# A graph layer's weight stage: seven combined block products replaced by four plain projections

## The chip, the core and the metric

The kernel runs on one core of a Trainium2 chip. The metric is the time of one execution on the device in microseconds (us); the times shown are medians over runs. The engines are named as the profile names them: PE is TensorE (matmuls), PEld its weight loads, DVE is VectorE, ACT is ScalarE, POOL is GpSimd, and SP is the engine that issues the DMA transfers. "L279" is line 279 of the kernel before.

## The reference

The input is 64 graphs of 256 nodes with 768 features, and for each a 256 x 256 matrix of 0 and 1. Each graph goes through a layer norm with a ReLU and then through one graph layer, whose result is added to the input:

```python
h = jnp.maximum(_layernorm(x, axis=-1), 0.0)
adj = heads.astype(hs.dtype)
radj = jnp.swapaxes(adj, 1, 2)
deg, rdeg = adj.sum(-1), radj.sum(-1)          # deg_c, rdeg_c: at least 1
ctx = jnp.matmul(adj, hs @ Wadj.T + badj) / deg_c[..., None]
ctx = ctx + jnp.matmul(radj, hs @ Wrev.T + brev) / rdeg_c[..., None]
ctx = ctx + hs @ Wself.T + bself
agg = jnp.einsum('bij,bijr->bir', adj, E[rels])
rel = agg @ Wr.T + br * deg[..., None]
...
return ctx + rel                                # x + this
```

With entries of 0 and 1 the relation terms come down to rows that depend on the degrees alone, so they become one small extra matmul. What is left is, for each graph, three 256 x 768 matrices (forward neighbour means, reverse neighbour means, and h itself), each times a 768 x 768 weight matrix, summed. This last part is called the weight stage below.

## The kernel before

The kernel works through the 64 graphs (`B`) in a software pipeline. `step(t)` works on three graphs at once: graph M = t is in the weight stage, A = t + 1 in the neighbour sums, and N = t + 2 is loaded and normalised. Each engine carries out its instructions in the order in which `step` writes them; the scheduler does not move them. A graph's 256 nodes are C = 2 blocks of 128 partitions, its 768 features are F = 6 blocks of 128, and FH = 3, HO = 384 are the halves.

For graph N, `load` (L159 to L163) fetches `x`, `adj` (both directions) and `xT`, an x that comes already transposed from the host. `degrees` (L171, ACT) casts adj to `a` and sums its rows; `statistics` (L181 to L194, DVE, with one small power on POOL, L184) makes mean, reciprocal deviation and degrees in `cols`. `spread` (L201) transposes `cols` on PE, copies it twice on ACT (`tokT`, `line`), and sends four rows through DRAM (`d<-line`, L208) and back to all partitions (`row<-d`, L210). `normalise` (L223 to L227) writes h as a pair of float32r tiles, `hi` and its remainder `lo`, with DVE and ACT taking turns.

For graph A, `aggregate(A, f)` makes one of six neighbour sums: four float32r matmuls of 512 columns (L248) into one of the two banks of `pa`, and a DVE multiply by the reciprocal degrees (L253) that reads the bank and writes two thirds of X's block f. `self_features` (L239 on POOL, L240 on ACT) normalises `xT` with `row` and writes the last third of X. X has two buffers, `pa` has two banks, `row`, `xT`, `adj`, `hi` and `lo` have one buffer each.

For graph M the weight stage treats X (2 x 2 blocks) times W (2 x 2 blocks) with seven block products in place of eight. `combine_weights` (L107 to L110, DVE, once) forms sums of weight blocks, `combine_left` (L270 to L273, POOL, every step) forms sums of blocks of X in place. Each `product` is 9 float32 matmuls of 384 columns (L279), in the trace two records each; four of the seven carry one more float32r matmul with `rows` and `tokT` (L285). Three products accumulate further onto a bank that another has already filled. `add_out` (L294) adds a bank to x, the last add (L351) takes one bank twice. Between the products `step` places the neighbour sums of A in three pairs. `prepare_rows` (once) builds `rows` out of biases and relation weights.

A flag counts entries of adj other than 0 and 1; a general path, not taken here, would then run after the main one.

Of the kernel before, what the change touches and what calls it, by code (L numbers as in the profile page):

```python
# [9 lines left out]
F32 = mybir.dt.float32  # L10
F32R = mybir.dt.float32r
# [3 lines left out]
ALU = mybir.AluOpType  # L15
AX = mybir.AxisListType

P = 128
# [5 lines left out]
def kernel(  # L24
# [24 lines left out]

    nc = tc.nc
    B, L, H = x.shape
    NREL = e_t.shape[1]
# [2 lines left out]
    F = H // P  # L59
    FH = F // 2  # L60
    HO = H // 2
# [17 lines left out]
    def main_path(main: ExitStack):  # L79
        pool1 = main.enter_context(tc.tile_pool(name="pool1", bufs=1))  # L80
# [3 lines left out]
        ps2 = main.enter_context(tc.tile_pool(name="ps2", bufs=2, space=bass.MemoryType.PSUM))  # L84
        ps1 = main.enter_context(tc.tile_pool(name="ps1", bufs=1, space=bass.MemoryType.PSUM))

        w11, w21, w22, t1, t2, t3, t4 = (
            pool1.tile([P, FH, 3, HO], F32, name=n) for n in ("w11", "w21", "w22", "t1", "t2", "t3", "t4")
        )
        rows = pool1.tile([P, 4, HO], F32R, name="rows")  # L90
        tok = [pool1.tile([P, C, NROW], F32, name=f"tok{i}") for i in range(2)]
        cols = [pool1.tile([P, C, 64], F32, name=f"cols{i}") for i in range(2)]

        def load_weights():
            def block(t, k, n):
                for s, w in enumerate((wadj_t, wrev_t, wself_t)):
                    v = w.rearrange("(f p) o -> p f o", p=P)
                    nc.sync.dma_start(t[:, :, s, :], v[:, k * FH : (k + 1) * FH, ts(n, HO)])

            block(w11, 0, 0)  # L100
            block(w21, 1, 0)
            block(t3, 0, 1)
            block(w22, 1, 1)

        def combine_weights():

            nc.vector.tensor_sub(t1, t3, w11)  # L107
            nc.vector.tensor_sub(t2, w22, t1)
            nc.vector.tensor_sub(t4, w21, t2)
            nc.vector.tensor_sub(t3, w22, t3)  # L110

        def prepare_rows():


            eT = pool1.tile([P, NREL], F32, name="eT")
            nc.sync.dma_start(eT, e_t)
            wr = [pool1.tile([P, H], F32, tag=f"hl{k}", name=f"wr{k}") for k in range(2)]
            nc.sync.dma_start(wr[0], wr_t)
            nc.sync.dma_start(wr[1], wrr_t)
            brow = pool3.tile([P, H], F32, tag="x", name="brow")  # L120
            nc.vector.memset(brow, 0.0)
            pick = pool1.tile([P, 2, P], F32, tag="s1", name="pick")
            nc.vector.memset(pick, 0.0)
            for q in range(4):
                nc.sync.dma_start(brow[q * 32 : q * 32 + NROW, :], bias)
                nc.vector.tensor_copy(pick[:, 0, q * 32 + 3 : q * 32 + 4], eT[:, 1:2])
                nc.vector.tensor_copy(pick[:, 1, q * 32 + 4 : q * 32 + 5], eT[:, NBASE + 1 : NBASE + 2])
            hi = pool1.tile([P, H], F32R, tag="hx", name="rows_hi")
            for n in range(2):
                pr = ps2.tile([P, 512], F32, tag="pa", name=f"pr{n}")  # L130
                for k in range(2):
                    nc.tensor.matmul(pr[:, :HO], pick[:, k, :], wr[k][:, ts(n, HO)], start=(k == 0), stop=(k == 1))
                nc.vector.tensor_add(brow[:, ts(n, HO)], brow[:, ts(n, HO)], pr[:, :HO])
            nc.vector.tensor_copy(hi, brow)
            hi = hi.bitcast(F32)
            nc.vector.tensor_sub(brow, brow, hi)
            nc.vector.tensor_copy(rows, brow[:, :1].unsqueeze(2).to_broadcast([P, 4, HO]))
            for q in range(4):
                at = slice(q * 32, (q + 1) * 32)
                src = (hi if q % 2 == 0 else brow)[at, :]  # L140
                zero = pick[at, 0, 16:17].to_broadcast([32, HO])
                c = q // 2

                for k, part in enumerate(((0, 0, 1), (1, 0, 1), (1, 1, 1), None)):
                    if part is None:
                        nc.vector.tensor_scalar(
                            rows[at, k, :], src[:, ts(1, HO)], 1.0 if c == 0 else -1.0, None, op0=ALU.mult
                        )
                    elif part[0] == c:
                        nc.vector.tensor_copy(rows[at, k, :], src[:, ts(part[1], HO)])  # L150
                    else:
                        nc.vector.tensor_copy(rows[at, k, :], zero)

        S = [{} for _ in range(B)]

# [98 lines left out]
                s["X"][:, f, 0:2, :].rearrange("p s i -> p (s i)"), pa, s["row"][:, 2:4, :].rearrange("p s i -> p (s i)")  # L254
            )

        def left(b):
            X = S[b]["X"]

            def block(c, k):  # L260
                return X[:, k * FH : (k + 1) * FH, :, ts(c, P)]

            return block(0, 0), block(0, 1), block(1, 0), block(1, 1)

        def combine_left(b):

            s = S[b]
            a11, a12, a21, a22 = left(b)
            s["s1"] = pool1.tile([P, FH, 3, P], F32, tag="s1", name=f"s1_{b}")
            nc.gpsimd.tensor_tensor(s["s1"], a21, a22, op=ALU.add)  # L270
            nc.gpsimd.tensor_tensor(a21, a11, a21, op=ALU.subtract)  # L271
            nc.gpsimd.tensor_tensor(a11, s["s1"], a11, op=ALU.subtract)  # L272
            nc.gpsimd.tensor_tensor(a12, a12, a11, op=ALU.subtract)  # L273

        def product(b, ps, l, w, start, stop=True, row=None):
            n = 0
            for f in range(FH):
                for k in range(3):
                    nc.tensor.matmul(  # L279
                        ps, l[:, f, k, :], w[:, f, k, :], start=(start and n == 0),  # L280
                        stop=(stop and row is None and n == 3 * FH - 1), skip_group_check=not start,
                    )
                    n += 1
            if row is not None:
                nc.tensor.matmul(  # L285
                    ps, S[b]["tokT"], rows[:, row, :], start=False, stop=stop, skip_group_check=not start
                )

        def bank(b, name, pool=None):
            return (pool or ps1).tile([P, 512], F32, tag=name, name=f"{name}_{b}")[:, :HO]  # L290

        def add_out(b, c, n, ps):
            o = S[b]["x"][:, c, ts(n, HO)]
            nc.vector.tensor_add(o, ps, o)  # L294

        def step(t):

            M, A, N = t, t + 1, t + 2
            has_m, has_a, has_n = 0 <= M < B, 0 <= A < B, 0 <= N < B
            if has_n:  # L300
                load(N)
            if t == -2:
                load_weights()
                prepare_rows()
                combine_weights()
            if has_a:
                new_left(A)
            if has_m:
                a11, a12, a21, a22 = left(M)
                p1 = bank(M, "p1", ps2)  # L310
                product(M, p1, a11, w11, True)
            if has_a:
                aggregate(A, 0)
                aggregate(A, 1)
            if has_m:
                add_out(M, 0, 0, p1)
                p2 = bank(M, "p2")
                product(M, p2, a12, w21, True, row=0)
                combine_left(M)
            if has_a:  # L320
                aggregate(A, 2)
                aggregate(A, 3)
                self_features(A)
            if has_n:
                degrees(N)
                statistics(N)
            if has_m:
                add_out(M, 0, 0, p2)
                p4 = bank(M, "p4")
                product(M, p4, a22, t4, True, row=1)  # L330
            if has_a:
                aggregate(A, 4)
                aggregate(A, 5)
            if has_m:
                add_out(M, 1, 0, p4)
                p5 = bank(M, "p5")
                product(M, p5, S[M]["s1"], t1, True, row=2)
            if has_n:
                spread(N)
            if has_m:  # L340
                add_out(M, 1, 1, p5)
                product(M, p1, a11, t2, False)
                add_out(M, 0, 1, p1)
            if has_n:
                normalise(N)
            if has_m:
                product(M, p5, a12, w22, False, row=3)
                add_out(M, 0, 1, p5)
                product(M, p1, a21, t3, False)
                o = S[M]["x"][:, 1, :].rearrange("p (n o) -> p n o", n=2)  # L350
                nc.vector.tensor_add(o, p1.unsqueeze(1).to_broadcast([P, 2, HO]), o)  # L351
                nc.sync.dma_start(out_v[M], S[M]["x"])

        for i in range(2):
# [171 lines left out]
```

## Time and profile before

| | |
|---|---|
| median of 3 runs | 3097.47 us |
| all runs | 3095.09 to 3099.42 us |
| the profiled execution's own time | 3099.42 us |
| its span, first to last instruction | 3097.4 us |
| mean granted clock of PE | 0.992 |
| float32 product records on PE (L279) | 8064, spread over three groups, 486 to 487 ns each |
| neighbour-sum matmuls (L248) | 1536, 398 to 422 ns each |
| row matmuls (L285) | 256, 633 ns each |
| combine_left on POOL (L270 to L273) | 256, 2618 to 2664 ns each |
| self_features on POOL (L239) | 128, 3652 ns each |
| DMA, mean over the span | 74 GB/s |

The durations of PE are those of single records. Records overlap, so these durations add up to more than the time PE is busy; what a record adds to a stream is the distance from its start to the next one's, and the chain of waits shows pieces that are free of overlap. In that chain each piece begins where the engine or transfer that released it ended. The time of an execution (3099.42) is 2.0 us longer than the span of its instructions (3097.4).

### The profile page before, as it was taken

What the parts mean: (1) busy time and instruction counts of PE and PEld (TensorE: products, weight loads), DVE (VectorE), ACT (ScalarE), POOL (GpSimd) and SP (SyncE); (2) the same over time, 40 slices, a digit from 0 to 9 for tenths busy, and PEclk for the clock granted to TensorE, in tenths of its full rate; (3) what the DMA queues carried; (4) which work ended last, traced back from release to release, by engine and by line L of the source; (5) the groups of instructions that cost most, each with busy time, mean ns of one, the idle gap of its engine ahead of it and who ended that gap; (6) DMA issues with size and microseconds to landing.
All of it is one profiled execution on the core that took longest, in us unless ns stands there. A gap on an engine that the chain in (4) does not pass through costs nothing.

```text
span 3097.4 us, 24497 instructions
## 1 busy us (share of the span) xinstructions
PE 3023.2 (98%) x9930; PEld 1875.4 (61%) x9930; DVE 1015.1 (33%) x1963; ACT 339.6 (11%) x833; POOL 1185.2 (38%) x454
## 2 busy tenths in 40 slices
PE   1999999999999999999999999999999999999999
PEld 1566666666666666666666666666666666666665
DVE  4433333333233333333333332332333333333331
ACT  0111011011011011110110110110111101101100
POOL 1434334344344344343343343443443443433432
PEclk7999999999999999999999999999999999999999
DMA  4222212212212212212222122122122122222210
GB/s 154 78 72 72 78 64 80 79 61 82 79 55 80 87 55 79 79 65 79 72 72 79 62 82 79 61 83 79 55 78 89 55 79 75 68 79 72 72 62 21
DMA packets 118029, 227.96 MB, mean 74 GB/s; under 512 B 6020, under 2 KB 60292, under 8 KB 117912
## 3 DMA queue, kind: packets, MB, share of 16 engines
q1 hardware_dynamic: 117912, 226.36, 21.3%
q8 instruction: 79, 1.29, 0.2%
q14 instruction: 38, 0.31, 0.0%
HBM read 175.74 MB, written 50.59 MB: 73 GB/s over the span
## 4 chain that ended last, share of the span: by engine, by line
PE 97%; issue 2%; DVE 0%; POOL 0%; DMA 0%; ACT 0%; SPq 0%; POOLq 0%; ACTq 0%
PE p L279 84%; PE pa L248 11%; PE p L285 1%; PE pt L201 0%; POOL xT L239 0%; DVE lo L227 0%; DMA row<-d 0%; DVE hx L223 0%; ACT hi L226 0%; ACT a L171 0%; POOL cols L184 0%; ACT X L240 0%; DMA d<-line 0%; DVE X L253 0%; DVE x L351 0%
## 5 line engine op out<-in xcount | busy, mean ns | idle before, releaser
L279 PE MATMUL p<-w,X 128*128 128x384 f32 x3456 | 1148.3, 487 | 0.0
L279 PE MATMUL p<-t,X 128*128 128x384 f32 x3456 | 1145.9, 486 | 0.0
L279 PEld LDWEIGHTS p<-w,X 128*128 128x128 f32 x3456 | 657.7, 190 | 448.2 <-issue 2.4
L279 PEld LDWEIGHTS p<-t,X 128*128 128x128 f32 x3456 | 650.5, 190 | 423.9
L272 POOL TENSOR_TENSOR X<-s,X 128x1152 f32<-128x1152 f32 x64 | 170.5, 2664 | 1159.0 <-PE p L279 1159.0
L253 DVE TENSOR_TENSOR X<-pa,row 128x512 f32<-128x512 f32 x384 | 259.0, 688 | 762.3 <-PE pa L248 760.5
L239 POOL TENSOR_TENSOR xT<-xT,row 128x1536 f32<-128x1536 f32 x128 | 467.5, 3652 | 12.2 <-DMA row<-d 7.2
L279 PE MATMUL p<-t,s 128*128 128x384 f32 x1152 | 381.9, 486 | 0.0
L294 DVE TENSOR_TENSOR x<-p,x 128x384 f32<-128x384 f32 x384 | 209.3, 552 | 379.2 <-PE p L279 347.3
L248 PE MATMUL pa<-a,hi 128*128 128x512 f32 x768 | 323.9, 422 | 2.1 <-ACT hi L226 2.1
L248 PE MATMUL pa<-a,lo 128*128 128x512 f32 x768 | 305.6, 398 | 3.4 <-DVE lo L227 3.4
L279 PEld LDWEIGHTS p<-t,s 128*128 128x128 f32 x1152 | 218.7, 190 | 141.3
L273 POOL TENSOR_TENSOR X<-X 128x1152 f32<-128x1152 f32 x64 | 170.0, 2655 | 322.9 <-PE p L279 322.9
L270 POOL TENSOR_TENSOR s<-X 128x1152 f32<-128x1152 f32 x64 | 167.6, 2618 | 320.5 <-PE p L279 306.5
L227 DVE SCALAR_TENSOR_TENSOR lo<-hx,cols,hi 128x768 fp32r<-128x768 f32 x128 | 134.0, 1047 | 451.6 <-ACT hi L226 451.6
L240 ACT ACTIVATE X<-xT 128x1536 f32<-128x1536 f32 x64 | 94.9, 1484 | 1619.6 <-POOL xT L239 1619.6
L248 PEld LDWEIGHTS pa<-a,hi 128*128 128x128 f32 x768 | 145.5, 189 | 54.8 <-ACT hi L226 3.1
L271 POOL TENSOR_TENSOR X<-X 128x1152 f32<-128x1152 f32 x64 | 168.1, 2626 | 5.0
L248 PEld LDWEIGHTS pa<-a,lo 128*128 128x128 f32 x768 | 145.4, 189 | 39.6 <-DVE lo L227 4.7
L285 PE MATMUL p<-rows,tokT 128*128 128x384 f32 x256 | 162.1, 633 | 0.0
L190 DVE TENSOR_SCALAR tok<-tok 128x4 f32<-128x4 f32 x64 | 10.9, 170 | 404.0 <-ACT a L171 404.0
L226 ACT ACTIVATE hi<-hx,cols 128x768 fp32r<-128x768 f32 x128 | 119.9, 936 | 107.9 <-DVE hx L223 107.9
(52 smaller groups left out, 787.7 us busy)
## 6 DMA issues: line engine op xcount, KB each, us to landing
x<-in_x_dram SPq DMA_DIRECT2D x64, 768.0 KB
xT<-in_x_t_dram SPq DMA_DIRECT2D x64, 768.0 KB
out_dram<-x SPq DMA_DIRECT2D x64, 768.0 KB
adj<-in_adj_dram SPq DMA_DIRECT2D x64, 512.0 KB
row<-d SPq DMA_DIRECT2D x64, 512.0 KB
d<-line SPq DMA_DIRECT2D x128, 2.0 KB
w<-in_Wadj_dram SPq DMA_DIRECT2D x3, 576.0 KB
w<-in_Wrev_dram SPq DMA_DIRECT2D x3, 576.0 KB
```

The lines of the kernel that those rows point to most:

```text
L226: nc.scalar.activation(s["hi"][:, c, :], hx[:, c, :], AF.Copy, scale=rstd)
L227: nc.vector.scalar_tensor_tensor(s["lo"][:, c, :], hx[:, c, :], rstd, s["hi"][:, c, :].bitcast(F32), op0=ALU.mult, op1=ALU.subtract)
L239: nc.gpsimd.tensor_tensor(xT, xT, row[:, k : k + 1, :].to_broadcast([P, F, L]), op=op)
L248: nc.tensor.matmul(pa, s[part][:, c, ts(f, P)], s["a"][:, c, :, :].rearrange("p s i -> p (s i)"), start=(k == 0), stop=(k == 2 * C - 1),)
L253: nc.vector.tensor_mul(s["X"][:, f, 0:2, :].rearrange("p s i -> p (s i)"), pa, s["row"][:, 2:4, :].rearrange("p s i -> p (s i)"))
L270: nc.gpsimd.tensor_tensor(s["s1"], a21, a22, op=ALU.add)
L271: nc.gpsimd.tensor_tensor(a21, a11, a21, op=ALU.subtract)
L272: nc.gpsimd.tensor_tensor(a11, s["s1"], a11, op=ALU.subtract)
L273: nc.gpsimd.tensor_tensor(a12, a12, a11, op=ALU.subtract)
L279: nc.tensor.matmul(ps, l[:, f, k, :], w[:, f, k, :], start=(start and n == 0), stop=(stop and row is None and n == 3 * FH - 1), skip_group ...
L285: nc.tensor.matmul(ps, S[b]["tokT"], rows[:, row, :], start=False, stop=stop, skip_group_check=not start)
L294: nc.vector.tensor_add(o, ps, o)
```

## The change

The block scheme of seven products goes. The three weight matrices are loaded whole (`w_sb`), in three transfers and not twelve, and no sums of weight blocks or of blocks of X are formed. For each of the 2 x 2 output blocks, `project` runs one row matmul and then 18 float32 matmuls into a bank of `po` (two banks), and adds the bank to x once. `rows` becomes 2 x 768 wide, without signs and half-width pieces. In `step`, the neighbour sums stand in two groups of three, and `spread` and `normalise` follow each other behind the third projection. The short name of the change speaks of neighbour sums in two float32r passes, transposes laid out by the host and row values spread by DMA; these parts are in both kernels, word for word.

```diff
-        w11, w21, w22, t1, t2, t3, t4 = (
-            pool1.tile([P, FH, 3, HO], F32, name=n) for n in ("w11", "w21", "w22", "t1", "t2", "t3", "t4")
-        )
-        rows = pool1.tile([P, 4, HO], F32R, name="rows")
+        w_sb = [pool1.tile([P, F, H], F32, name=f"w{k}") for k in range(3)]
+        rows = pool1.tile([P, 2, H], F32R, name="rows")
...
+            for t, w in zip(w_sb, (wself_t, wadj_t, wrev_t)):
+                nc.sync.dma_start(t, w.rearrange("(f p) o -> p f o", p=P))
-        def combine_weights():
-            nc.vector.tensor_sub(t1, t3, w11)
-            nc.vector.tensor_sub(t2, w22, t1)
-            nc.vector.tensor_sub(t4, w21, t2)
-            nc.vector.tensor_sub(t3, w22, t3)
...
-            nc.vector.tensor_copy(rows, brow[:, :1].unsqueeze(2).to_broadcast([P, 4, HO]))
             for q in range(4):
                 at = slice(q * 32, (q + 1) * 32)
                 src = (hi if q % 2 == 0 else brow)[at, :]
-                for k, part in enumerate(((0, 0, 1), (1, 0, 1), (1, 1, 1), None)):
...
+                for c in range(2):
+                    if c == q // 2:
+                        nc.vector.tensor_copy(rows[at, c, :], src)
                     else:
+                        nc.vector.tensor_copy(rows[at, c, :], pick[at, 0, 16:17].to_broadcast([32, H]))
...
-        def combine_left(b):
-            nc.gpsimd.tensor_tensor(s["s1"], a21, a22, op=ALU.add)
-            nc.gpsimd.tensor_tensor(a21, a11, a21, op=ALU.subtract)
-            nc.gpsimd.tensor_tensor(a11, s["s1"], a11, op=ALU.subtract)
-            nc.gpsimd.tensor_tensor(a12, a12, a11, op=ALU.subtract)
-        def product(b, ps, l, w, start, stop=True, row=None):
...
+        def project(b, c, n):
+            s = S[b]
+            po = ps2.tile([P, 512], F32, tag="po", name=f"po_{b}_{c}_{n}")[:, :HO]
+            nc.tensor.matmul(po, s["tokT"], rows[:, c, ts(n, HO)], start=True, stop=False)
+            for f in range(F):
                 for k in range(3):
                     nc.tensor.matmul(
+                        po, s["X"][:, f, k, ts(c, P)], w_sb[(k + 1) % 3][:, f, ts(n, HO)],
+                        start=False, stop=(f == F - 1 and k == 2),
                     )
+            o = s["x"][:, c, ts(n, HO)]
+            nc.vector.tensor_add(o, po, o)
...
             if has_m:
-                a11, a12, a21, a22 = left(M)
-                p1 = bank(M, "p1", ps2)
-                product(M, p1, a11, w11, True)
+                project(M, 0, 0)
             if has_a:
-                aggregate(A, 0)
-                aggregate(A, 1)
+                for f in range(3):
+                    aggregate(A, f)
             if has_m:
-                add_out(M, 0, 0, p1)
-                p2 = bank(M, "p2")
-                product(M, p2, a12, w21, True, row=0)
-                combine_left(M)
+                project(M, 0, 1)
             if has_a:
-                aggregate(A, 2)
-                aggregate(A, 3)
+                for f in range(3, 6):
+                    aggregate(A, f)
                 self_features(A)
             if has_n:
                 degrees(N)
                 statistics(N)
             if has_m:
-                add_out(M, 0, 0, p2)
-                p4 = bank(M, "p4")
-                product(M, p4, a22, t4, True, row=1)
-            if has_a:
-                aggregate(A, 4)
-                aggregate(A, 5)
-            if has_m:
-                add_out(M, 1, 0, p4)
-                p5 = bank(M, "p5")
-                product(M, p5, S[M]["s1"], t1, True, row=2)
+                project(M, 1, 0)
             if has_n:
                 spread(N)
-            if has_m:
-                add_out(M, 1, 1, p5)
-                product(M, p1, a11, t2, False)
-                add_out(M, 0, 1, p1)
-            if has_n:
                 normalise(N)
             if has_m:
-                product(M, p5, a12, w22, False, row=3)
-                add_out(M, 0, 1, p5)
-                product(M, p1, a21, t3, False)
-                o = S[M]["x"][:, 1, :].rearrange("p (n o) -> p n o", n=2)
-                nc.vector.tensor_add(o, p1.unsqueeze(1).to_broadcast([P, 2, HO]), o)
+                project(M, 1, 1)
                 nc.sync.dma_start(out_v[M], S[M]["x"])
```

More of the change, by code (lines that the diff above doesn't have):

```diff
@@ L94, in load_weights @@
         def load_weights():
[L95 to L103, printed above, removed]
-        def combine_weights():
-            nc.vector.tensor_sub(t1, t3, w11)
-            nc.vector.tensor_sub(t2, w22, t1)
-            nc.vector.tensor_sub(t4, w21, t2)
-            nc.vector.tensor_sub(t3, w22, t3)
+            for t, w in zip(w_sb, (wself_t, wadj_t, wrev_t)):
+                nc.sync.dma_start(t, w.rearrange("(f p) o -> p f o", p=P))
         def prepare_rows():
@@ L140, in prepare_rows @@
                 src = (hi if q % 2 == 0 else brow)[at, :]
-                zero = pick[at, 0, 16:17].to_broadcast([32, HO])
-                c = q // 2
-                for k, part in enumerate(((0, 0, 1), (1, 0, 1), (1, 1, 1), None)):
[L145 to L150, printed above, removed]
+                for c in range(2):
+                    if c == q // 2:
+                        nc.vector.tensor_copy(rows[at, c, :], src)
                     else:
-                        nc.vector.tensor_copy(rows[at, k, :], zero)
+                        nc.vector.tensor_copy(rows[at, c, :], pick[at, 0, 16:17].to_broadcast([32, H]))
         S = [{} for _ in range(B)]
@@ L255, in aggregate @@
             )
[L257 to L263, printed above, removed]
-        def combine_left(b):
-            s = S[b]
-            a11, a12, a21, a22 = left(b)
-            s["s1"] = pool1.tile([P, FH, 3, P], F32, tag="s1", name=f"s1_{b}")
-            nc.gpsimd.tensor_tensor(s["s1"], a21, a22, op=ALU.add)
-            nc.gpsimd.tensor_tensor(a21, a11, a21, op=ALU.subtract)
-            nc.gpsimd.tensor_tensor(a11, s["s1"], a11, op=ALU.subtract)
-            nc.gpsimd.tensor_tensor(a12, a12, a11, op=ALU.subtract)
-        def product(b, ps, l, w, start, stop=True, row=None):
-            n = 0
-            for f in range(FH):
+        def project(b, c, n):
+            s = S[b]
+            po = ps2.tile([P, 512], F32, tag="po", name=f"po_{b}_{c}_{n}")[:, :HO]
+            nc.tensor.matmul(po, s["tokT"], rows[:, c, ts(n, HO)], start=True, stop=False)
+            for f in range(F):
                 for k in range(3):
                     nc.tensor.matmul(
-                        ps, l[:, f, k, :], w[:, f, k, :], start=(start and n == 0),
-                        stop=(stop and row is None and n == 3 * FH - 1), skip_group_check=not start,
-                    )
[L283 to L294, printed above, removed]
+                        po, s["X"][:, f, k, ts(c, P)], w_sb[(k + 1) % 3][:, f, ts(n, HO)],
+                        start=False, stop=(f == F - 1 and k == 2),
+                    )
+            o = s["x"][:, c, ts(n, HO)]
+            nc.vector.tensor_add(o, po, o)
         def step(t):
@@ L304, in step @@
                 prepare_rows()
-                combine_weights()
             if has_a:
```

## The prediction, made before the changed kernel ran

> **What bounds the kernel now.** I read the page first: busy time by engine and the shares of the chain that ended last.
>
> ```profile
> PE 3023.2 (98%) x9930; PEld 1875.4 (61%) x9930; DVE 1015.1 (33%) x1963; ACT 339.6 (11%) x833; POOL 1185.2 (38%) x454
> ...
> PE 97%; issue 2%; DVE 0%; POOL 0%; DMA 0%; ACT 0%; SPq 0%; POOLq 0%; ACTq 0%
> ```
>
> TensorE carries 97% of the chain, and no other engine is busy for 40% of the span. A high busy share alone proves little (see the skill below), so next I took the chain of waits of one whole step in the middle (start in us, length in us, what).
>
> ```profile
> 1502.81 1.86 PE pa L248 x8
> 1504.67 5.81 PE p L279 x18
> 1510.48 0.17 PE p L285
> 1510.65 1.87 PE pa L248 x8
> ...
> 1526.34 0.11 PE pt L201
> 1526.45 11.61 PE p L279 x36
> 1538.06 0.18 PE p L285
> ```
>
> The reader is to see that one piece begins where the last ends: no wait, no issue gap. Hence the prices on TensorE: a float32 record of the products takes 11.61/36 = 0.3225 us (a float32 matmul leaves two records), a neighbour-sum matmul 1.86/8 = 0.233, a row matmul 0.17, the transpose 0.11. A step is 126 x 0.3225 + 24 x 0.233 + 4 x 0.174 + 0.11 = 47.03 us. The windows view over 1502.36 to 1549.39 gives the same period, with TensorE busy for 47.03 of 47.03 us and the granted clock at 1.00. The kernel is bound by the count of TensorE records, and by nothing else after the first 93 us.
>
> The start is the other part that counts. There the timeline shows VectorE as the engine everything waits for (from 41.63 us on it is never idle until the statistics are out, while the windows view has no DMA traffic at all from 30 to 40 us):
>
> ```profile
> 35.92 0.96 DVE L137 CAST rows<-brow 128x1536 fp32r<-128x1536 f32 x1
> ...
> 41.63 3.76 DVE L107 TENSOR_TENSOR t<-t,w 128x3456 f32<-128x3456 f32 x1
> ...
> 52.89 3.75 DVE L110 TENSOR_TENSOR t<-w,t 128x3456 f32<-128x3456 f32 x1
> 56.55 1.01 DVE L181 BATCH_NORM_STATS2 stats<-x 128x6 f32<-128x384 f32 x2
> ```
>
> and then TensorE's first step with a product:
>
> ```profile
> 78.98 8.26 PE L279 MATMUL p<-w,X 128*128 128x384 f32 x18
> 86.78 0.69 PE L248 MATMUL pa<-a,hi 128*128 128x512 f32 x1
> ...
> 90.88 0.80 PE L248 MATMUL pa<-a,lo 128*128 128x512 f32 x1 [2.87 <-DVE lo L227]
> ```
>
> From 78.98 to the start of p2 at 93.38 in the chain are 14.4 us, where the steady prices of p1 and eight sums give 5.81 + 1.86 = 7.67. So 6.7 us are lost there: some 2.3 in p1 itself (granted clock 0.50 from 78 to 82 us), the rest on the wait for `lo` and the slow clock after it.
>
> **What the Trainium skill says.** "FP8 and Floating Point Precision", section TensorE Precision Notes: true float32 makes four passes through the array. Agrees: a float32 matmul of 384 columns takes 2 x 0.3225 = 0.645 us, the float32r row matmul of the same width 0.17. "TensorE: Matmul & The Clock Gate", section "Wait — 56ns, not 53.3ns?": columns over 2.4 GHz and about 2.5 ns more. For two passes of 384 that is 322.5 ns, which the trace has; for 512 columns of float32r it would be 216 ns and the trace has 233, so I use 233. The same page, Part 1, says that the array's clock drops to half after some 3.4 us of idling; the 0.50 after the idle 5.4 us before the transpose at 78.74 agrees. "Perfetto Trace Analysis" (its opening note) warns that matmul busy time is a bad metric because matmuls overlap; here the records' mean of 487 ns exceeds their spacing of 322.5, so only spacings are summed.
>
> **The change, part by part.** The three things first named in its short title (float32r passes over split h, transposed x from the host, row values by DMA) are in the kernel before already: `hi` and `lo` at L248, `in_x_t_dram`, the transfers `d<-line` and `row<-d`. They move nothing. What changes is the weight stage.
>
> *Products.* Seven products of 9 matmuls become four projections of 18: 72 instead of 63, 144 records instead of 126. Each has the same shape (128x128 weights, 384 float32 columns), so 18 x 0.3225 = 5.806 us a step, and 64 steps: +371.6 us. All of it lies on the chain. The row matmuls stay four a step, only first in their group instead of last; in the steady chain neither switching between float32 and float32r nor back costs anything beyond the prices above.
>
> *Sum groups.* The sums ran in three pairs, and `pa` has two banks; now they run in two groups of three, so the third of each group must wait until VectorE has read the first. The step before the first product shows this wait at full clock, since there four and then two sums follow each other:
>
> ```profile
> 70.46 0.69 DVE L253 TENSOR_TENSOR X<-pa,row 128x512 f32<-128x512 f32 x1 [1.01 <-PE pa L248]
> ...
> 71.20 0.19 PEld L248 LDWEIGHTS pa<-a,hi 128*128 128x128 f32 x1 [0.28 <-DVE X L253]
> 71.20 0.50 PE L248 MATMUL pa<-a,hi 128*128 128x512 f32 x1
> 71.31 0.19 PEld L248 LDWEIGHTS pa<-a,lo 128*128 128x128 f32 x1
> ...
> 71.54 0.39 PE L248 MATMUL pa<-a,lo 128*128 128x512 f32 x1
> ```
>
> VectorE starts 0.20 after a bank's last matmul ends and takes 0.69; the next sum takes 4 x 0.233 = 0.93. The reader is to see 0.34 us between the two starts 71.20 and 71.54 instead of 0.233: 0.11 late. VectorE is free at that moment in the new order too: the add into x runs from 0.20 to 0.75 us after the projection, the first sum is read from 1.13. I take 0.115 us, twice a step, 63 steps: +14.5. Bounds: 0 (released just in time) and 0.23 (twice).
>
> *combine_left on GpSimd.* Four operations of 2.6 us a step go, 676 us of POOL time in all. They hold the release of no TensorE wait in the steady chain, so 0 there. GpSimd is then left with self_features (7.4 us) and the small power.
>
> *Adds.* Seven products were drained by six adds of 0.55 us and one of 0.96, now four of 0.55. VectorE is at 15.4 us of 47: 0, except the last of the run (0.96 to 0.55): -0.4.
>
> *Order of spread, statistics and normalise.* TensorE now meets the transpose after the third projection, some 41 us into a step. What it needs: the last sum is read at about 30.3; statistics took 4.15 us plus 0.5 for its last four operations plus the power; done near 35.5, so nearly 6 us of cover. `row` then lands some 6.6 us later (ScalarE copies, `d<-line` 1.2, `row<-d` 4.5, from the chain at the start), under a projection of 11.8 us, and is wanted by the sums after a further one. normalise needs about 5 us (in the middle step from 1538.6 to 1543.2) and has 23. SP's order stays x, adj, xT, d, row, out; its xT load waits for ScalarE's relu, which comes earlier as GpSimd waits for no product. Cost 0.
>
> *Weights at the start.* combine_weights goes: 41.63 to 56.55 on VectorE, on the path to the first statistics: -14.9. Rows: 5.71 us (35.92 to 41.63) for a full-width copy and sixteen pieces of 32x384 become eight of 32x768; a 768-wide cast of this kind took 0.56 (L134), the 384-wide pieces follow at about 0.3, so 4.0 to 4.7: -1.5. Twelve loads become three with the same 7.1 MB; the windows show 371 to 375 GB/s there, the queue stays full: 0, bounds -3 and +1.
>
> *First product step.* p00 has 36 records, 11.6 us and 2.3 for the slow clock, and covers normalise of the next batch even if that takes as long as before (finished 11.9 us after p1 began). So of 6.7 lost, 4.4 come back: -4.4.
>
> Sum against the profiled span: 3097.4 + 371.6 + 14.5 - 14.9 - 1.5 - 4.4 - 0.4 = 3462.3. That execution took 3099.42, 2.0 more than its span, and lies 1.95 above the median 3097.47; the two cancel, so the median should come to about 3462 us.
>
> **The rivals.**
> 1. The third sum is released in time and no bank wait appears: 3462.3 - 14.5 = 3448. For it: only 0.11 us are missing, and an earlier add moves nothing there. Against: the start shows the same spacing late.
> 2. A new wait takes hold: the transpose comes late, because statistics and the power sit behind the third sum group on in-order engines and TensorE has the third projection alone as cover. The 6 us of cover have to be used up first; from there each us costs 62, so 1 us gives 3524. For it: a reciprocal chain over ACT, DVE and POOL. Against: the sum above, and GpSimd is emptier.
> 3. Not slower: float32 records of before are held back by GpSimd rewriting X under the loads, and run faster once combine_left is gone. It would decide from (47.03 - 6.4 - 0.23)/144 = 0.2806 us a record, with the time at 3097 less the start's 21, about 3076. Against: in the chain the 36 records from 1526.45, run at one spacing though GpSimd works below the first half (L270, L271, up to 1531.6) and is idle below the second; so do the 18 from 1504.67. Nothing speaks for it but that it isn't excluded for weights in another layout.
>
> **How the numbers follow.** Forecast 0.74, rival 1 0.13, rival 2 0.11, rival 3 0.02. The range holds the forecast with its bounds (bank wait up to 0.23: +14.5; start -3 to +1) and rival 1: 3446 to 3478. A measurement of this kernel can tell about 0.2%, 6 us, from no change. Slower 0.98; rival 3 is split, 0.01 faster and 0.01 within.
>
> **What would show it.** The chain of a middle step: 36 records in 11.61 us four times, period near 53.1 us (52.85 without bank waits). TensorE's waits: about 0.1 us on VectorE before the third and sixth sum, none at the transpose. First product near 62.5 us instead of 79. It is wrong if records are spaced other than 0.3225, or if a step has a wait over 0.5 us.

## The result, and the profile after

The changed kernel takes 3462.2 us (median of 4 runs, 3461.84 to 3463.59), the kernel before 3097.21 us in the same comparison. The ratio is 1.1179, with a 95% interval from 1.116 to 1.1199: slower by 365 us. The forecast was 3462 us in a range of 3446 to 3478.

The busy times and the shares of the chain, from the page of the kernel after:

```profile
PE 3408.0 (98%) x11082; PEld 2087.7 (60%) x11082; DVE 832.9 (24%) x1758; ACT 353.2 (10%) x833; POOL 504.1 (15%) x198
...
PE 98%; DMA 1%; SPq 0%; DVE 0%; POOL 0%; ACT 0%; issue 0%; POOLq 0%
```

TensorE has 1152 instructions more and the same share of a longer span; VectorE and GpSimd have lost 182 and 681 us of work, and of this only what lay on the path at the start will show in the time. The chain of waits over one step in the middle of the kernel after (start in us, length in us, what; L237 are the projections, L222 the sums, L234 the rows, L175 the transpose; the view ends at 1510 us, so its last line is cut short):

```profile
1454.73 2.91 PE pa L222 x12
1457.65 0.17 PE po L234
1457.82 11.61 PE po L237 x36
...
1484.12 0.11 PE pt L175
1484.23 0.17 PE po L234
1484.41 11.61 PE po L237 x36
...
1507.80 2.22 PE pa L222 x9
```

The reader is to see 36 records in 11.61 us, to the last digit what they took before, and no gap at the transpose or in front of a projection. From the first line to the last is one step: 1507.80 - 1454.73 = 53.07 us, against 47.03 before. One piece is not what it was: twelve sums take 2.91 us, where twelve times the old spacing of 0.233 is 2.80. The timeline of the kernel after, at such a group, shows why (start, length, instruction, idle time before it and what ended it):

```profile
1508.77 0.69 DVE L227 TENSOR_TENSOR X<-pa,row 128x512 f32<-128x512 f32 x1 [0.37 <-PE pa L222]
...
1509.51 0.19 PEld L222 LDWEIGHTS pa<-a,hi 128*128 128x128 f32 x1 [0.29 <-DVE X L227]
1509.52 0.50 PE L222 MATMUL pa<-a,hi 128*128 128x512 f32 x1
...
1509.86 0.40 PE L222 MATMUL pa<-a,lo 128*128 128x512 f32 x1
```

VectorE reads the first bank until 1509.46. Only then does the weight load for the third sum start, and the first two matmuls of that sum stand 0.34 us apart in place of 0.233. The start, in the chain of waits of the kernel after:

```profile
39.67 1.03 DVE stats L155 x2
...
62.34 12.65 PE po L237 x36
75.00 2.92 PE pa L222 x12
```

The first statistics begin at 39.67 and not 56.55, the first projection at 62.3 where the first product began at 78.98, and the sums follow the projection without a wait for `lo`.

### The profile page after: what moved, and what is told of

Read it like the earlier page. It is cut to its first block, busy times and chain, and to the rows that moved or that the text cites. A ratio compares the mean times of both kernels' runs of the same rounds, so it can differ in the third digit from the quotient of the medians.

```text
span 3460.1 us, 26192 instructions
## 1 busy us (share of the span) xinstructions
PE 3408.0 (98%) x11082; PEld 2087.7 (60%) x11082; DVE 832.9 (24%) x1758; ACT 353.2 (10%) x833; POOL 504.1 (15%) x198
## 4 chain that ended last, share of the span: by engine, by line
PE 98%; DMA 1%; SPq 0%; DVE 0%; POOL 0%; ACT 0%; issue 0%; POOLq 0%
PE po L237 86%; PE pa L222 11%; PE po L234 1%; DMA wr<-in_Wr_dram 0%; PE pt L175 0%; POOL xT L213 0%; SPq L92 0%; SPq L98 0%; PE pr L114 0%; DMA row<-d 0%; DVE rows L126 0%; DVE rows L124 0%; DVE stats L155 0%; ACT a L145 0%; POOL cols L158 0%
## 5 line engine op out<-in xcount | busy, mean ns | idle before, releaser
L237 PE MATMUL po<-w,X 128*128 128x384 f32 x9216 | 3014.8, 487 | 0.0
L237 PEld LDWEIGHTS po<-w,X 128*128 128x128 f32 x9216 | 1751.6, 190 | 1164.1 <-issue 0.9
L242 DVE TENSOR_TENSOR x<-po,x 128x384 f32<-128x384 f32 x256 | 142.9, 558 | 2320.6 <-PE po L237 2320.6
L222 PE MATMUL pa<-a,hi 128*128 128x512 f32 x768 | 355.9, 463 | 2.1 <-ACT hi L200 2.1
L158 POOL TENSOR_TENSOR cols<-cols,half 128x2 f32<-128x2 f32 x64 | 64.2, 1003 | 1989.4 <-DVE cols L157 1989.4
L222 PE MATMUL pa<-a,lo 128*128 128x512 f32 x768 | 305.0, 397 | 0.5 <-DVE lo L201 0.5
L222 PEld LDWEIGHTS pa<-a,hi 128*128 128x128 f32 x768 | 145.5, 190 | 79.2 <-DVE X L227 36.9
L222 PEld LDWEIGHTS pa<-a,lo 128*128 128x128 f32 x768 | 145.8, 190 | 41.3 <-DVE lo L201 1.5
L145 ACT ACTIVATE a<-adj 128x256 fp32r<-128x256 int32 x256 | 103.2, 404 | 445.6 <-DMA adj<-in_adj_dram 445.6
L155 DVE BATCH_NORM_STATS2 stats<-x 128x6 f32<-128x384 f32 x256 | 126.4, 536 | 0.0
L234 PE MATMUL po<-rows,tokT 128*128 128x384 f32 x256 | 111.6, 436 | 0.0
L197 DVE TENSOR_SCALAR hx<-x,cols 128x768 f32<-128x768 f32 x128 | 78.3, 612 | 0.0
L234 PEld LDWEIGHTS po<-rows,tokT 128*128 128x128 f32 x256 | 48.6, 190 | 25.7 <-issue 11.3
L145 ACT ACTIVATION_READ_ACCUMULATOR a<-adj 128x1 f32 x256 | 47.8, 187 | 0.0
```

The source lines that it names most:

```text
L145: nc.scalar.activation(s["a"][:, c, k, :], s["adj"][:, c, k, :], AF.Copy, accum_out=tok[b % 2][:, c, 4 - k : 5 - k])
L155: nc.vector.bn_stats(stats[:, c, n, :], s["x"][:, c, ts(n, HO)])
L197: nc.vector.tensor_scalar(hx[:, c, :], s["x"][:, c, :], v[:, c, MEAN : MEAN + 1], 0.0, op0=ALU.subtract, op1=ALU.max)
L222: nc.tensor.matmul(pa, s[part][:, c, ts(f, P)], s["a"][:, c, :, :].rearrange("p s i -> p (s i)"), start=(k == 0), stop=(k == 2 * C - 1),)
L234: nc.tensor.matmul(po, s["tokT"], rows[:, c, ts(n, HO)], start=True, stop=False)
L237: nc.tensor.matmul(po, s["X"][:, f, k, ts(c, P)], w_sb[(k + 1) % 3][:, f, ts(n, HO)], start=False, stop=(f == F - 1 and k == 2),)
```

## The experiments

**The bank wait alone.** The changed kernel with a third bank for the sums:

```diff
+        ps3 = main.enter_context(tc.tile_pool(name="ps3", bufs=3, space=bass.MemoryType.PSUM))
...
-            pa = ps2.tile([P, 512], F32, tag="pa", name=f"pa_{b}_{f}")
+            pa = ps3.tile([P, 512], F32, tag="pa3", name=f"pa_{b}_{f}")
```

> The changed kernel with three PSUM banks for the neighbour sums in place of two. My theory: the third sum of each group waits 0.11 us for its bank, twice a step in 63 steps, so twelve sum matmuls come down from 2.91 to 2.80 us in the chain and the time from 3462.2 to about 3448.5 us (-13.9). Rival (the late start of the third sum comes from something else than the bank, such as the multiply by row or the order on VectorE): no change, 3462 us.

Measured: 3448.16 us (3447.22 to 3449.7), 14.0 below the changed kernel's 3462.2 (timed on another occasion: the kernel before came out at 3097.21 us beside the one and at 3095.88 beside the other); ratio to the kernel before 1.1134 (1.1118 to 1.1149). The chain of waits of this run:

```profile
1502.69 2.80 PE pa L223 x12
1505.49 0.17 PE po L235
1505.66 11.61 PE po L238 x36
```

Twelve sums are back at 2.80 us. The wait for the bank was the whole of the difference, and its price is the 0.11 us that a group grew by. It is not the idle time that the waits view (idle time of each engine, by what ended it) of the changed kernel gives for it: there TensorE's weight loads wait 36.9 us on VectorE in 128 cases (0.29 each), but most of that lies under a running matmul.

**The count of matmuls alone.** The changed kernel with half of the last projection left out:

```diff
-            for f in range(F):
+            nf = FH if (c, n) == (1, 1) else F
+            for f in range(nf):
...
-                        start=False, stop=(f == F - 1 and k == 2),
+                        start=False, stop=(f == nf - 1 and k == 2),
```

> The changed kernel with 9 of its 72 projection matmuls a step left out (the second half of the features in the last projection), so 126 records a step as in the seven-product kernel; the output lacks that part. My theory (only the count of records matters): 3462.2 - 64 x 18 x 0.3225 = 3090.6 us, that is 6 to 7 us below the kernel before, by its shorter start less the bank waits. Rival (a record of one scheme costs more than one of the other, by weight layout, by the in-place sums or by accumulation over banks): at least 1% away, under 3060 or over 3120 us.

Measured: 3091.14 us (19 runs, 3089.58 to 3092.41) against 3095.88 for the kernel before, ratio 0.9983 (0.9977 to 0.999). Nine matmuls a step are worth 3462.2 - 3091.1 = 371.1 us. At an equal count the two kernels differ by 0.2%, in the direction of the shorter start.

The other way round, the kernel before with an eighth product:

```diff
                 product(M, p1, a21, t3, False)
+                product(M, p1, a22, w11, False)
```

> The kernel before with an eighth product of 9 matmuls added at the end of every step, onto a bank that is already in use; the output has that product in it too. My theory: 18 records of 0.3225 us in 64 steps, all on the chain: 3097.2 + 371.6 = 3468.8 us, which is the changed kernel's time with another start and no bank waits. Rival (some of the added matmuls hide in idle time of TensorE): clearly less than 3440 us.

Measured: 3468.4 us (3467.28 to 3472.31) against 3095.8, so 372.6 us for nine matmuls a step; ratio 1.12 (1.1183 to 1.1218). None of the added matmuls hid anywhere. The two runs together also decide the prediction's third rival, a "not slower" outcome: a record costs the same in both schemes.

**GpSimd's in-place sums alone.** The kernel before without `combine_left`:

```diff
-                combine_left(M)
...
-                product(M, p5, S[M]["s1"], t1, True, row=2)
+                product(M, p5, a21, t1, True, row=2)
```

> The kernel before without the four GpSimd sums of blocks of X in each step; the product that used their sum takes a block of X instead, so the output is that of other operands. My theory: GpSimd's 676 us were hidden and only the first step gains, a few us from the wait for lo: 3092 to 3097 us. Rival 3 of the prediction (the float32 records are slowed by GpSimd working beside them): records spaced below 0.3225 us and a time well below 3090, down to 2750 us at 0.28.

Measured: 3095.06 us against 3095.88, ratio 0.9994 (0.9986 to 1.0003): no difference that can be told, and 36 product records in the middle of the run still take 11.61 us. In the steady part GpSimd's sums were hidden. The first step does change. The timeline of the kernel before, and then that of this run, at the second half of the second graph's normalise:

```profile
82.86 3.21 POOL L271 TENSOR_TENSOR X<-X 128x1152 f32<-128x1152 f32 x1
83.52 2.97 DVE L223 TENSOR_SCALAR hx<-x,cols 128x768 f32<-128x768 f32 x1
...
87.39 2.62 POOL L272 TENSOR_TENSOR X<-s,X 128x1152 f32<-128x1152 f32 x1 [1.32 <-PE p L279]
87.50 3.33 DVE L227 SCALAR_TENSOR_TENSOR lo<-hx,cols,hi 128x768 fp32r<-128x768 f32 x1 [1.00 <-ACT hi L226]
```

```profile
84.25 0.61 DVE L223 TENSOR_SCALAR hx<-x,cols 128x768 f32<-128x768 f32 x1
85.86 1.02 DVE L227 SCALAR_TENSOR_TENSOR lo<-hx,cols,hi 128x768 fp32r<-128x768 f32 x1 [1.00 <-ACT hi L226]
```

Beside GpSimd's sums the two VectorE operations take 2.97 and 3.33 us, without them 0.61 and 1.02. This is what made TensorE wait for `lo` in its first step. Without it, the stretch from the transpose in front of the first product to the start of the second product is 9.4 us (80.66 to 90.01) and not 14.6 (78.74 to 93.38). In this run's profile the transpose itself came 1.9 us later; the one before it, ahead of any product, was already 2.2 us late (62.97 and 60.78), so this is not the work of the sums. The second product starts 3.4 us earlier and the profiled span is 3.9 us shorter (3093.5 and 3097.4). The medians differ by only 0.8: the profiled execution of the kernel before was the slowest of its first four, and how much a median run gains in the first step stays open.

**The weight sums at the start alone.** The kernel before without `combine_weights`:

```diff
-                combine_weights()
...
-                product(M, p4, a22, t4, True, row=1)
+                product(M, p4, a22, w21, True, row=1)
...
-                product(M, p5, S[M]["s1"], t1, True, row=2)
+                product(M, p5, S[M]["s1"], w11, True, row=2)
...
-                product(M, p1, a11, t2, False)
+                product(M, p1, a11, w22, False)
```

> The kernel before without the four VectorE subtractions of weight blocks at the start; the products use loaded blocks instead, so the output is that of other weights. My theory: these 14.9 us are on the path to the first statistics, the first product starts at about 64 us and not 79, and the time is 3097.2 - 14.9 = 3082.3 us. Rival (another engine or transfer is late anyway at the start): less than 5 us gained, 3092 us or more.

Measured: 3083.44 us against 3095.88, ratio 0.9955 (0.9941 to 0.9969), 12.4 us with an uncertainty of about 4. The profiled spans differ by 13.9 us (3097.4 and 3083.5), and the second product starts at 78.73 and not at 93.38. The subtractions were on the path; their 14.9 us came back nearly whole.

**How much cover the transpose has.** Extra VectorE work in front of the statistics of the changed kernel, in 62 steps, one operation and then three:

```diff
+        scr = pool1.tile([P, 3456], F32, name="scr")
+        nc.vector.memset(scr, 1.0)
...
         def statistics(b):
             s = S[b]
+            if b >= 2:
+                for _ in range(3):
+                    nc.vector.tensor_sub(scr, scr, scr)
```

> The changed kernel with one extra VectorE subtraction of 128x3456 (3.76 us) ahead of the statistics in every step but the first two. My theory: the statistics chain has about 7 us of cover before TensorE's transpose (ready at 1529.7 or a little later, wanted at 1536.7), so nothing changes: 3462 us. Rival (the order of statistics and the third projection is already on the edge): 3.76 x 62 = 233 us more at the most, 3695 us, or a part of it.

> The same with three extra subtractions (11.3 us). My theory: the cover of about 7 us is used up and TensorE waits some 4.2 us at each transpose, 62 times: 3462 + 260 = 3722 us (3660 to 3760 for a cover of 6.5 to 8). Rival (the cover is larger, since the scheduler of TensorE's queue or the other engines absorb the delay): below 3600 us.

Measured: one operation 3462.99 us (3462.9 to 3463.47), no change. Three operations 3839.43 us (3838.87 to 3840.38), 377 more than the changed kernel, where 260 were expected. The chain of waits of the run with three (L155 the extra work, L180 the transpose):

```profile
3638.05 2.93 PE pa L227 x12
...
3655.59 1.00 POOL cols L163
3656.60 0.04 issue
3656.64 0.47 PE pt L180
3657.12 0.32 PE po L239
3657.44 12.74 PE po L242 x36
3670.18 0.18 PE po L239
3670.36 11.61 PE po L242 x36
```

The chain now leaves TensorE, runs over VectorE and the power on GpSimd, and comes back at the transpose. The reader is to see what comes after the wait: transpose 0.47 and not 0.11, rows 0.32 and not 0.17, and a projection of 12.74 us where the next takes 11.61. The windows view of the same run, over one wait in the middle and the 4 us after it (length, busy time of PE, PEld, DVE, ACT and POOL, granted clock, DMA share, GB/s):

```profile
1523.00:1527.00 4.00, 0.29 (x2) 0.29 (x3) 3.86 (x16) 0.00 (x0) 0.99 (x1) 0.91 0.00 0
1527.00:1529.00 2.00, 2.00 (x5) 1.31 (x5) 0.69 (x3) 1.27 (x3) 0.00 (x0) 0.50 0.00 1
1529.00:1531.00 2.00, 2.00 (x6) 1.10 (x5) 1.39 (x2) 0.57 (x1) 0.00 (x0) 0.83 0.14 52
```

TensorE waits 3.89 us a step at the transpose (251.6 us in 63 cases by the waits view, of which 10.5 belong to the first graph), 241 us in all. The other 136 us, 2.2 a step, go with the half clock that is granted after nearly every wait: the mean granted clock of the run is 0.960 against 0.997, and (1 - 0.960) x 3836.9 less (1 - 0.997) x 3460.1 is 143 us. The price of one wait is not fixed. Two waits of equal length, each with the projection behind it (L180 the transpose, L242 the projection):

```profile
108.25 0.33 PE L180 MATMUL pt<-ident,cols 128*128 128x128 f32 x1 [3.89 <-POOL cols L163]
108.60 11.77 PE L242 MATMUL po<-w,X 128*128 128x384 f32 x36
...
165.44 0.47 PE L180 MATMUL pt<-ident,cols 128*128 128x128 f32 x1 [3.89 <-POOL cols L163]
166.03 14.32 PE L242 MATMUL po<-w,X 128*128 128x384 f32 x36
```

After the first the clock stayed at 1.00 (windows view, 108 to 114 us) and the projection took what it always takes; after the second the clock was 0.50 from 166 to 170 us and the projection took 2.55 us more. The three extra operations delay the statistics by 11.25 us (from 1511.68 to 1522.93), so the cover was 11.25 - 3.89, about 7.4 us.

**Another start for the seven products.** The runs without the in-place sums and without the weight sums point at the start, and at a seven-product version that should beat both kernels. First, the first graph's statistics, spread and normalise go ahead of the weight sums and the rows:

```diff
             if t == -2:
                 load_weights()
-                prepare_rows()
-                combine_weights()
...
                 self_features(A)
+            if t == -1:
+                prepare_rows(*late)
...
                 normalise(N)
+            if t == -2:
+                late.extend(load_rows())
+                combine_weights()
```

`load_rows` holds the transfers that stood in `prepare_rows`; it loads into a buffer of X, and GpSimd clears `brow`, which VectorE did before. `late` carries its tiles to `prepare_rows`.

> The seven-product kernel with another start: the first graph's statistics, spread and normalise come before the weight sums and the making of rows on VectorE, and row's transfer before the loads for rows on SP; all else is as before. My theory: VectorE is idle from 2 to 28 us in the kernel before and row lands only at 68 us; with row landing at 30 to 35 us the first product should start at 50 to 60 us instead of 79, so 3070 to 3080 us, faster than both kernels. Rival (VectorE's 15 us of weight sums and 12 us of rows stay on the path whatever the order): 3090 us or more.

Measured: 3084.21 us (3083.21 to 3086.62), ratio 0.9962 (0.9949 to 0.9976): faster than both, by less than expected. VectorE was still the path, with the weight sums up to 42.7 us (the last of them took 6.97 us beside GpSimd's work on `xT`, in place of 3.76, and that work 13.85 in place of 7.05) and the rows from 47.5 to 59.1. So the loads for rows moved ahead of the weights, the rows to the time in which the weights still land, and two of the four sums behind the second graph's normalise (the edit is against the run just described):

```diff
             if t == -2:
-                load_weights()
+                late = load_rows()
+                load_weights(0)
...
-            if t == -1:
-                prepare_rows(*late)
...
             if t == -2:
-                late.extend(load_rows())
-                combine_weights()
+                load_weights(1)
+                prepare_rows(*late)
+                combine_weights(0)
+            if t == -1:
+                combine_weights(1)
```

> The seven-product kernel with the start rearranged further: the loads for rows stand ahead of the weights, row's transfer stands between the two halves of the weights, rows are made while the weights still land, and the last two weight sums come after the second graph's normalise. My theory: in the run with the early start VectorE was the path (weight sums up to 42.6 us, rows up to 59.1), so taking rows and two sums off it brings the first product from 63 to about 46 us and the time from 3084.2 to about 3067 us (3060 to 3075). Rival (the slow clock, row's transfer or the in-place sums of the first step take what is gained): 3078 us or more.

Measured: 3072.22 us (3071.16 to 3073.02) against 3096.32, ratio 0.992 (0.9907 to 0.9934). The chain of waits of this run:

```profile
60.13 0.94 ACT hi L233
61.09 2.30 DVE lo L234
63.44 2.50 PE pa L255 x5
65.94 7.01 PE p L286 x18
```

The second product starts at 65.94 where it started at 93.38 before. The first began at 52.5, not at the expected 46, and TensorE still waits for `lo`, which takes 2.30 us beside GpSimd's in-place sums. This is the fastest version of the study. The changed kernel was not given such a start, so what it would gain is not shown.

## Why the prediction was right, point by point

*Products, +371.6.* Right, and shown alone from both sides: 371.1 taken out of the changed kernel, 372.6 added to the kernel before.

*Sum groups, +14.5.* Right: 14.0 by the run with three banks, 2 x 63 x 0.11 = 13.9 by the chain. One place at the start of the old trace already held the two-bank loop at full clock, which made this a reading and not a guess. Rival 1 (no wait) is out.

*combine_left, 0 in the steady chain.* Right, 0.8 us within an uncertainty larger than that. Rival 3 (records slowed by GpSimd) is out.

*Weight sums and rows at the start, -14.9 and -1.5.* Right in sum: the first statistics moved by 56.55 - 39.67 = 16.9. The rows gave 5.71 - 4.13 = 1.6. The transfer of the relation table landed 1.6 us earlier, inside the bounds of -3 to +1, and the two small matmul sums behind it took 1.4 more, so the fewer, larger loads brought 0.4 us in the end (the first write of `rows` at 35.54 and not 35.92).

*First step, -4.4.* The mechanism was right, the wait for `lo` is gone and the slow clock remains. The size was a little off in the profiled run: 2.3 us were put down to the slow clock, and the first projection took 12.65 - 11.61 = 1.0 more than a later one. In three other runs with the same first step (63 matmuls, three banks, one delay) it took 13.67, 14.13 and 14.09, that is 2.1 to 2.5 more. The windows view shows the difference: from 64 to 66 us the granted clock was 0.92 in the profiled run and 0.60, 0.50 and 0.50 in those three. So the price of the slow clock depends on the execution, and 2.3 us was near what it usually is. What the prediction did not see is why `lo` had been late in the kernel before. It named the wait, but not that GpSimd stretched VectorE's operations.

*Order of spread and statistics, 0.* Right; the waits view of the kernel after has no TensorE wait at the transpose beyond the first two graphs. The cover was put at nearly 6 us and measured as about 7.4. The price of rival 2 was wrong at this size of wait: 62 us for each us of delay counts the wait alone. The run with three extra operations shows 377 us for 3.89 us of wait, 97 for each, since the slow clock after it has to be paid as well. What a shorter wait costs was not measured, apart from the 0.11 us at the bank.

*Adds, -0.4.* Right: the last add took 0.56 in place of 0.96.

*The sum.* The forecast of 3462 and the median of 3462.2 agree more closely than the terms do, and that is luck. The sum for the profiled span was 3462.3 and the span is 3460.1: the first step came out 1.0 to 1.3 us lower than forecast, the bank wait 0.6 and the statistics at the start 0.5. Executions of the kernel before lie between 3094.1 and 3100.4. A hit within a few us is what the terms support.

## What to carry to other kernels

Where TensorE is packed, sum the spacings of its records in the chain, not their durations nor its busy share, and price a change by the count of records; work that other engines no longer do is worth nothing there. Then look at the start by itself: it is run once, but it is a chain of other engines, and here rearranging it was worth 24 us while 676 us of GpSimd work in the steady part were worth none. When consecutive uses of a resource grow from two to three with two buffers, check the loop time (matmuls, start of the reader, reading, release) against the time of one use.

## What the runs showed of the hardware

A wait of 3.89 us on TensorE cost about 6.1 us a step on average, since the clock was granted at half after it; in the step shown it was 0.50 for some 2 us and 0.83 for the next 2. Waits of the same length did not cost the same: after one the clock stayed at 1.00, after another it was 0.50 for 4 us. The wait of 0.11 us for a bank left the clock at 1.00.

VectorE and GpSimd slowed each other with some operations: VectorE's 0.61 became 2.97 us, 1.02 became 3.33, 3.76 became 6.97, and GpSimd's 7.05 became 13.85. The Trainium skill, "SBUF — State Buffer", section "SBUF: two separate sides", tells of a pair of ports that the two share as an exclusive lock, held for a whole instruction. The trace agrees as far as it goes: the operation of 2.97 us that begins at 83.52 ends at 86.49, shortly after GpSimd's of 82.86 to 86.07, as if it had waited for that one to end; the slow `lo` operations of 81.40 and 87.50 both end 0.82 us after the GpSimd operations that began just before them (at 83.60 and 90.83, against 82.78 and 90.01). That the lock is the cause was not tried by itself. Not every pair did so: beside GpSimd's `xT` work the batch-norm statistics of the kernel before kept their 1.01 us (at 1513.16).
